# A relational graph layer on one core: a relu moved to VectorE, one-hots moved into the table stage, 15 scattered tiles, a new order

## The chip, the core and the metric

The kernel runs on one core of one Trainium2 chip. A core has TensorE (PE, matrix products, which accumulate in PSUM), VectorE (DVE), ScalarE (ACT), GpSimd (POOL, which here mostly issues indirect DMAs), SyncE (SP, which issues the other DMAs) and 16 DMA engines. Each engine works through its own instructions in their written order; semaphores let it wait for others. The metric is the time of the whole program on the device in microseconds, the median of several runs. A profile is one execution; its span reaches from the first to the last instruction.

## What is computed

A graph with 625 nodes and 20625 edges (each drawn edge both ways, and a loop at every node), sorted by target, four kinds of edge, 512 features. In short:

```python
h = relu(layernorm(x))
for r in range(4):
    msg += (h[src] @ W_rel[r] + b_rel[r]) * where(edge_type == r, edge_weight, 0)
agg = segment_sum(msg, dst) / maximum(segment_sum(edge_weight, dst), 1)
x1  = layernorm(h + h @ W_self + b_self + agg) * g1 + b1
ffn = gelu(x1 @ W_ffn1 + b_ffn1) @ W_ffn2 + b_ffn2
out = x + layernorm(x1 + ffn) * g2 + b2
```

## The kernel before, in words

The nodes lie in five blocks of 128 rows (0 and 4 are called outer, 1 to 3 inner). The edges lie in 162 tiles of 128, sorted by target, so each tile reaches one or two blocks.

**Table stage.** Each block is centred and passed through a relu (`pre_norm`, the rest of the norm is a scale that follows later), transposed on TensorE (L406), copied to SBUF by ScalarE (L412), and multiplied with each of the four `W_rel`: 20 steps, `step = r * NB + i`, one table row of 128 x 512 each (`table_rows`, L463, eight passes on TensorE in fp32). In the steps of the first kind the next block's transposes stand in the middle of a row's products. VectorE scales each product, adds the bias (the eviction, L476) and SP stores it to `table` in DRAM. In `pre_norm` blocks 0 and 1 take their relu on VectorE (L427), blocks 2 to 4 on ScalarE (L423, L424). The relu of block `i + 3` is written behind step `i`, block 2's ahead of step 0.

**Outer blocks.** The edges of the outer blocks are not gathered. Their weights are summed into matrices (edges of one kind and source block against target), which multiply the table rows. Most of these tiles are scattered to DRAM cells: VectorE sums equal neighbours (`line_sums`, L732 to L740, eight columns at a time), GpSimd issues one indirect DMA for each tile (`scatter`, L746), and the matrix of each outer block is loaded back later (`load_sums`, L766, into `sums_w`). `LINES = 999, 16` gives the most tiles that are scattered for block 0 (31 here) and block 4 (16). The remaining outer tiles go through one-hots on VectorE (`node_hots`, L641 and L651, named `os` and `od`), scaling on ScalarE (L659, `ohw`) and short products (L673), a few of them already at steps 15 to 17.

**Degrees and first edges.** Weighted degrees come from bf16 one-hots (`degree_hots`, L839) times weights. Those of the 30 inner groups are made at steps 8 and 9; from them come counts (L972) and, on TensorE, the group in which each inner block's first edge stands (`first_edges`, L903 to L907, `x_group`, at step `FIRST_AT = 16`). GpSimd then loads these edges (`load_first_edges`, L911). The one-hots of the 72 outer degree tiles are made in two instructions behind the last table row (`outer_degree_hots`), in the memory of the feed-forward's two `gT` buffers.

**Edge stage.** GpSimd gathers the table row of every inner edge tile (L1313, 99 of them, and three first edges, L1391) into ten `ms` buffers. Three neighbouring tiles form a group: ScalarE weights the first (L1319), VectorE adds the next two (L1349), the sum is split in a high part (ScalarE, L1323) and a low part (VectorE, L1327), and TensorE adds both to the targets by a one-hot (L1374). In between TensorE has the self products (L501), the outer blocks' sums over the table (L1490, 40 of them, most on rows that SP loads back, L1485), the transposes (L406) and the feed-forward (L1055, L1075). The last block's norm and feed-forward end the program.

**What sets the order.** In the table stage the order is that of the written loop with its step constants. In the edge stage each piece of work is an `op` of a planner, and `ORDER`, a table of op numbers, is the order in which they are written out on all engines. GpSimd's stream is: the scatters as their weights come, at `FIRST_AT` the three loads, the last five scatters, an instruction that waits for the stored rows (L761), then the gathers.

Of the kernel before, what the change touches and what calls it, by code (L numbers as in the profile page):

```python
# [9 lines left out]
F32 = mybir.dt.float32  # L10
F32R = mybir.dt.float32r
I32 = mybir.dt.int32
BF16 = mybir.dt.bfloat16
# [3 lines left out]
P = 128  # L17
# [1 line left out]
NEAR = 63  # L19
PAUSE = 200  # L20
PIECE = 8
LINES = 999, 16


class EdgePlan:
# [48 lines left out]


ORDER = [
# [30 lines left out]
]  # L107


# [92 lines left out]
def gnn_layer(ctx, tc, x, edges, edge_line, edge_groups, w_self, w_rel, w_ffn1, w_ffn2, rows_in, bf_in, out, n_edges):  # L202
# [12 lines left out]
    nc = tc.nc  # L215
# [11 lines left out]
    NC = R * NB  # L227
# [191 lines left out]
    rx = const.tile([P, NB, 3], F32, name="rx")  # L419

    def pre_norm(i, mean):
        if i > 1:
            nc.scalar.activation(rx[:, i, 2:3], mean, AF.Copy, scale=-1.0)  # L423
            nc.scalar.activation(z[:, i, :], xs[:, i, :], AF.Relu, bias=rx[:, i, 2:3])  # L424
        else:
            for c in (slice(0, D // 2), slice(D // 2, D)) if i == 0 else (slice(0, D),):
                nc.vector.tensor_scalar(z[:, i, c], xs[:, i, c], mean, 0.0, op0=ALU.subtract, op1=ALU.max)  # L427
        nc.vector.tensor_scalar(rx[:, i, 0:1], var_of[i], EPS, None, op0=ALU.add)
        rsqrt_pow(rx[:, i, :])
# [138 lines left out]
    sums_w = {}  # L568
# [193 lines left out]

    def load_sums(i):
        b = lines[i][0]
        sums_w[b] = const.tile([P, NC, P], F32, name=f"sums_w{b}")
        load = (nc.sync if i else nc.scalar).dma_start(  # L766
            sums_w[b], cells[i][:P * NC * P, :].rearrange("(p c n) o -> p c (n o)", p=P, c=NC))
        if i:
            wait_for(load, made_row[-1:], "rows go first")
        wait_for(load,  # L770
                 scattered[i][:-1], "all cells are there")

    rdeg = const.tile([P, NB], F32, name="rdeg")
    W = ep.width
    starts = early.tile([P, -(-NT // 8), 8], F32, name="starts")
# [83 lines left out]
    dg = early.tile([4, NP], F32, name="dg")  # L859

    box_dg = {}

    def outer_degree_hots(j0, nj, oc):
        oc.append(buffer("gT").rearrange("p f q -> p (f q)").bitcast(BF16)[:, :nj * W].rearrange("p (j w) -> p j w", w=W))
        degree_hots(j0, nj, oc[0])

    def outer_degree_sums(j0, nj, oc):

        upper = ep.first[outer_blocks[2]] - 2 * P
        for j in range(j0, j0 + nj):  # L870
            s = ep.starts[deg_tiles[j]]
            lo, hi = max(s, 0), min(s + W, N)
            low = deg_tiles[j] < GROUP0
# [2 lines left out]
            if j == GROUPS:  # L876
                box_dg["p"] = buffer("ps")
                nc.tensor.matmul(box_dg["p"][:4, :], zeros[:, :4], zeros, start=True, stop=False)
            nc.tensor.matmul(box_dg["p"][:4, at:at + hi - lo], w3[:, j, :], oc[0][:, j - j0, lo - s:hi - s],
                             start=False, stop=j == ND - 1)  # L880

    def outer_degree_copy():
# [269 lines left out]
    FIRST_PIECE = 4  # L1152
    COLUMNS_AT, LINE_AT, DEGREE_HOTS_AT = (0, 2, 4, 7, 10, 12, 14), 9, (8, 9)
    COLUMNS_OF_EDGES_AT, LOAD_AT, LIMITS_AT = 5, 16, (3, 6)
    DEGREES_AT, SPREAD_AT, FIRST_AT = 13, 15, 16
    chunks = [(j0, min(DG, GROUPS - j0)) for j0 in range(0, GROUPS, DG)]
    ODG = -(-(ND - GROUPS) // GT)
    outer_chunks = [(j0, min(ODG, ND - j0)) for j0 in range(GROUPS, ND, ODG)]
    later_groups = [(a, min(2, NE - a)) for a in range(0, NE, 2)]
    pieces = [(0, 0, FIRST_PIECE)]  # L1160
# [20 lines left out]
    with tc.manual_schedule(engines={PE, DVE, ACT, mybir.EngineType.Pool}):  # L1181
# [12 lines left out]
        for r in range(R):  # L1194
            for i in range(NB):
# [26 lines left out]
                if step in DEGREE_HOTS_AT:  # L1222
                    j0, nj = chunks[DEGREE_HOTS_AT.index(step)]
                    hots.append((step, degree_hots(j0, nj, early.tile([P, nj, W], BF16, tag="oc", name=f"oc_{j0}", bufs=2))))
                if step in ADDS_AT:
                    for b in range(*((0, 2), (2, 4), (4, NB))[ADDS_AT.index(step)]):
                        nc.vector.tensor_add(xs[:, b, :], xs[:, b, :], b2_bc)
# [51 lines left out]

    rows_of_first = op("DVE", 2.2, first_rows, rank=(0.3,), level=0.2)  # L1280
    first_ready = op("DVE", 2.7, first_found, after=[rows_of_first], rank=(0.3,), level=0.2)
    degree_op, hots_ops = None, []
    for j0, nj in outer_chunks:
        oc = []
        h = op("DVE", 1.6, lambda j0=j0, nj=nj, oc=oc: outer_degree_hots(j0, nj, oc), take=["gT"], rank=(0.3,), level=0.2)
        first_sum = degree_op is None
        degree_op = op("PE", 0.028 * nj + 0.1, lambda j0=j0, nj=nj, oc=oc: outer_degree_sums(j0, nj, oc),
                       after=[h, degree_op], take=["ps"] if first_sum else [], give=[("gT", h)], lag=0.25, rank=(2, 0.05), level=0.3)
        sum_op = degree_op if first_sum else sum_op
    degree_op = op("ACT", 0.6, outer_degree_copy, after=[degree_op], take=["ow"], give=[("ps", sum_op)],  # L1290
                   rank=(2, 0.05))
    spread_op = op("PE", 0.4, outer_degree_rows, after=[degree_op], take=["ps"], give=[("ow", degree_op)], lag=0.25, rank=(2, 0.05), level=0.3)
    degree_op = op("DVE", 0.55, outer_degrees, after=[spread_op], give=[("ps", spread_op)], rank=(0.3,), level=0.2)
# [196 lines left out]
        nc.tensor.matmul(acc[b,], sums_w[b][:, c, :], kept[(b, c) if (b, c) in kept else c], start=first, stop=last)  # L1490

    landed = op("cells", CELLS, None)
    banked, before_ = [op("SP", 0.3, lambda: load_sums(1), after=[landed], lag=6.5, rank=(0, -1))], None
    for i, (k0, n_) in enumerate(later_groups):
        box = {}
        rank = (0.55, i)
# [273 lines left out]
```

## Time and profile before

| | |
|---|---|
| median of 3 runs | 259.22 us (258.03 to 260.24) |
| profiled execution | 259.05 us, its span 257.3 us |
| busy in the span: PE / DVE / ACT / POOL | 240.7 / 198.6 / 107.1 / 171.3 us |
| PE weight loads busy | 141.7 us |
| table stage on PE | 6.0 to 85.9 us |
| gathers issued on POOL | 92.7 to 225.7 us |
| DMA, mean over the span | 231 GB/s |

Times inside the profile count from the start of the span. In a row of the timeline stand the start, the busy time, the engine, the line, the operation with output and input, their sizes, the number of merged instructions, and in brackets the idle time of the engine ahead of it with what ended it; "issue" there means that nothing in the profile was waited for. A row of stretches gives for each engine the busy time and the number of instructions, then TensorE's granted clock (1.00 is full), the DMA engines' share and GB/s. Groups of the page list the line, the engine, the operation, the count, the busy time with the mean of one in ns, and the idle time ahead of them. PE is TensorE's products, PEld its weight loads, which lie beside them.

### The profile page before, as it was taken

Reading aid. Unit: us, or ns where it says so; the run is one execution under the profiler, and the core shown is the slowest. Engines: PE = TensorE matmul, PEld = TensorE weight load, DVE = VectorE, ACT = ScalarE, POOL = GpSimd, SP = SyncE. Lnnn points to the kernel's source line nnn. Section 1 sums busy time; section 2 is a strip of 40 time slices with the busy share of each in tenths; the row PEclk is TensorE's granted clock in tenths of the full one; section 3 lists DMA queues with packets and bytes.
Section 4 is the critical chain, followed back from the end, with each engine's and each line's share of the span. In section 5 each row is a group of like instructions: output and inputs, shape, how many; then the busy total and the mean of one; then the engine's idle time right before and its main releaser. Section 6 shows DMA issues by size and latency. Waiting matters only on the chain.

```text
span 257.3 us, 3583 instructions
## 1 busy us (share of the span) xinstructions
PE 240.7 (94%) x1049; PEld 141.7 (55%) x1049; DVE 198.6 (77%) x471; ACT 107.1 (42%) x328; POOL 171.3 (67%) x232
## 2 busy tenths in 40 slices
PE   7699999999989997999999998999996999899992
PEld 7245444444444663446454556666766748647871
DVE  2756699999897991699997979998695994977342
ACT  3132900000033001977462447855646672652540
POOL 5385588688888877877777677777777777701000
PEclk9979999999999999999999999999999999999998
DMA  5999899786263259998999977766777667821111
GB/s 179 349 408 406 318 347 326 283 311 248 85 203 127 83 158 338 384 349 302 300 321 357 321 201 207 206 200 197 199 213 206 202 204 206 241 87 41 43 41 43
DMA packets 24030, 59.44 MB, mean 231 GB/s; under 512 B 4452, under 2 KB 8776, under 8 KB 22855
## 3 DMA queue, kind: packets, MB, share of 16 engines
q0 software_dynamic: 9760, 26.79, 33.9%
q1 hardware_dynamic: 13920, 30.91, 33.6%
q10 hardware_dynamic: 326, 1.48, 1.7%
q8 instruction: 9, 0.15, 0.2%
q14 instruction: 15, 0.11, 0.1%
HBM read 49.99 MB, written 9.17 MB: 230 GB/s over the span
## 4 chain that ended last, share of the span: by engine, by line
PE 52%; DVE 17%; DMA 15%; issue 5%; POOL 4%; ACT 4%; SPq 1%; DVEq 0%; POOLq 0%; ACTq 0%
PE ps L463 24%; DMA ms<-table,row_i 12%; PE acc L1490 7%; PE ps L1055 6%; PE acc L1374 5%; PE ps L501 4%; POOL ms L1313 4%; PE ps L1075 3%; DVE add L1349 3%; DMA line<-in_edge_line_dram 2%; DVE z L489 2%; DVE gT L839 1%; DVE oh L1366 1%; DVE el L1327 1%; PE ps L406 1%
## 5 line engine op out<-in xcount | busy, mean ns | idle before, releaser
L1313 POOL DMA_INDIRECT ms<-table,row_i x99 | 98.5, 994 | 31.5 <-issue 14.0
L463 PE MATMUL ps<-wr,T 128*128 128x512 f32 (+2 forms) x168 | 72.8, 587 | 2.5 <-ACT T L412 2.5
L746 POOL DMA_INDIRECT cells<-weight,cell x47 | 49.2, 1046 | 14.8 <-DVE weight L740 7.6
L463 PEld LDWEIGHTS ps<-wr,T 128*128 128x128 f32 x168 | 31.3, 195 | 37.5 <-issue 30.7
L1349 DVE SCALAR_TENSOR_TENSOR add<-ms,wgt_g,add 128x512 f32<-128x512 f32 x55 | 40.4, 751 | 8.4 <-DMA ms<-table,row_i 5.1
L1055 PEld LDWEIGHTS ps<-T,w_sb 128*128 128x128 f32 x320 | 39.0, 191 | 5.8 <-issue 2.4
L1055 PE MATMUL ps<-T,w_sb 128*128 128x128 f32 (+2 forms) x320 | 39.7, 275 | 1.4 <-ACT gT L1061 1.1
L1075 PE MATMUL ps<-w_sb,gT 128*128 128x512 f32 (+2 forms) x96 | 37.0, 523 | 0.1
L1490 PE MATMUL acc<-tr,sums_w 128*128 128x512 f32 x60 | 29.5, 597 | 0.0
L1319 ACT ACTIVATE add<-ms,wgt_g 128x512 f32<-128x512 f32 x30 | 20.6, 689 | 19.0 <-DVE el L1327 13.8
L1075 PEld LDWEIGHTS ps<-w_sb,gT 128*128 128x128 f32 x96 | 16.4, 190 | 12.5 <-issue 9.8
L1374 PE MATMUL acc<-eh,oh 128*128 128x512 f32 x34 | 17.5, 530 | 5.1 <-ACT eh L1323 2.0
L1327 DVE TENSOR_TENSOR el<-add,eh 128x512 fp32r<-128x512 f32 x25 | 17.0, 684 | 4.9 <-ACT eh L1323 2.9
L1323 ACT CAST eh<-add 128x512 fp32r<-128x512 f32 x25 | 14.6, 584 | 12.3 <-DVE add L1349 12.2
L501 PE MATMUL ps<-ws_sb,T 128*128 128x512 f32 x40 | 18.8, 597 | 0.0
L659 ACT ACTIVATE ohw<-os,w 128x128 fp32r<-128x128 f32 x32 | 10.2, 389 | 19.4 <-DVE os L641 19.4
L1061 ACT ACTIVATE gT<-ps,bf 128x128 f32<-128x128 f32 (+1 forms) x40 | 13.9, 360 | 10.1 <-PE ps L1055 9.8
L476 DVE SCALAR_TENSOR_TENSOR tr<-ps,rx,brel_bc 128x512 f32<-128x512 f32 x15 | 11.1, 745 | 8.0 <-PE ps L463 5.9
L1374 PE MATMUL acc<-el,oh 128*128 128x512 f32 x34 | 17.1, 512 | 0.0
L1490 PEld LDWEIGHTS acc<-tr,sums_w 128*128 128x128 f32 x60 | 10.8, 189 | 8.3 <-issue 7.4
L1337 ACT ACTIVATE eh<-ms,ed 128x512 fp32r<-128x512 f32 x9 | 6.3, 712 | 21.0 <-issue 16.7
L1374 PEld LDWEIGHTS acc<-eh,oh 128*128 128x128 f32 x34 | 6.4, 189 | 12.6 <-ACT eh L1337 4.2
(250 smaller groups left out, 310.2 us busy)
## 6 DMA issues: line engine op xcount, KB each, us to landing
tr<-table SPq DMA_DIRECT2D x11, 512.0 KB, 6.2
w_sb<-in_L_gnn_W_ffn_dram SPq DMA_DIRECT2D x2, 2048.0 KB, 8.0
table<-tr SPq DMA_DIRECT2D x15, 256.0 KB, 2.8
wr<-in_L_gnn_W_rel_dram SPq DMA_DIRECT2D x3, 1024.0 KB, 7.4
cells<-zeros SPq DMA_DIRECT2D x2, 1280.0 KB, 8.2
ms<-table,row_i POOLq DMA_INDIRECT x99, 3.9
rows<-in_rows_dram SPq DMA_DIRECT2D x1, 1280.0 KB
sums_w<-cells ACTq DMA_DIRECT2D x1, 1280.0 KB
```

The source lines that it names most:

```text
L463: nc.tensor.matmul(p_[:, :h.stop - h.start], hT[i][:, k, :], wr_sb[r][:, k, h], start=(k == 0), stop=(k == KD - 1))
L501: nc.tensor.matmul(p[0], hT[i][:, k, :], ws_sb[:, k, :], start=(k == 0), stop=(k == KD - 1))
L746: s = nc.gpsimd.indirect_dma_start(out=cells[i][:, :], out_offset=bass.IndirectOffsetOnAxis(ap=cell[i][:, k:k + 1], axis=0), in_=weight[i] ...
L1055: nc.tensor.matmul(pu[:, low:nn + first], w1_sb[:, k, f * P:(f + 1) * P], x1T_b()[:, k, low:nn + first], start=(k == 0), stop=(k == KD - 1))
L1075: nc.tensor.matmul(po[h][:n, :w], box["gT"][:, f, at], w2_sb[:, f, c], start=(f == 0), stop=(f == KF - 1))
L1313: nc.gpsimd.indirect_dma_start(out=ms[j], out_offset=None, in_=table[:, :], in_offset=bass.IndirectOffsetOnAxis(ap=row_i[:, j:j + 1], axis=0))
L1319: nc.scalar.activation(box["sum"], ms[j], AF.Copy, scale=wgt_g[:, (j - GROUP0) // EG, 0:1])
L1323: nc.scalar.copy(box["high"], box["sum"])
L1327: nc.vector.tensor_sub(box["low"], box["sum"], box["high"].bitcast(F32))
L1349: nc.vector.scalar_tensor_tensor(to, ms[j], wgt_g[:, k, q:q + 1], box["sum"], op0=ALU.mult, op1=ALU.add)
L1374: nc.tensor.matmul(acc[bs], w.bitcast(F32) if of.dtype == F32 else w, of, start=first, stop=last)
L1490: nc.tensor.matmul(acc[b,], sums_w[b][:, c, :], kept[(b, c) if (b, c) in kept else c], start=first, stop=last)
```

## The change

Four things change. Block 2's relu is taken on VectorE like those of blocks 0 and 1. At most 15 tiles of block 4 are scattered instead of 16, so one tile more goes through one-hots. The outer degrees' one-hots are made at steps 17 and 18 of the table stage, in the memory of the second outer block's matrix (`sums_w`, which is now allocated for both blocks ahead of the stages), the 72 degree products become one op, and the second matrix's load comes behind that op. `FIRST_AT` goes from 16 to 17. `ORDER` is another table of the same 699 numbers (three ops go with the outer one-hots, three come with the 17th one-hot tile).

```diff
-LINES = 999, 16
+LINES = 999, 15
...
 ORDER = [
-    401, 403, 406, 411, 25, 2, 440, 27, 4, 441, 404, 405, 407, 32, 442, 420, 443, 408, 414, 3, 26, 28, 444, 5, 445, 6,
+    398, 400, 403, 408, 440, 441, 401, 7, 22, 0, 402, 404, 24, 2, 407, 23, 25, 29, 8, 3, 409, 1, 442, 34, 39, 443,
...
     def pre_norm(i, mean):
-        if i > 1:
+        if i > 2:
             nc.scalar.activation(rx[:, i, 2:3], mean, AF.Copy, scale=-1.0)
...
+    for b, _, _ in lines:
+        sums_w[b] = const.tile([P, NC, P], F32, name=f"sums_w{b}")
...
-    def outer_degree_hots(j0, nj, oc):
-        oc.append(buffer("gT").rearrange("p f q -> p (f q)").bitcast(BF16)[:, :nj * W].rearrange("p (j w) -> p j w", w=W))
-        degree_hots(j0, nj, oc[0])
-
-    def outer_degree_sums(j0, nj, oc):
+    outer_hots = sums_w[lines[1][0]].rearrange("p c n -> p (c n)").bitcast(BF16)[:, :(ND - GROUPS) * W].rearrange(
+        "p (j w) -> p j w", w=W)
+
+    def outer_degree_sums():
...
-    DEGREES_AT, SPREAD_AT, FIRST_AT = 13, 15, 16
+    DEGREES_AT, SPREAD_AT, FIRST_AT, OUTER_HOTS_AT = 13, 15, 17, (17, 18)
...
+                if step in OUTER_HOTS_AT:
+                    j0, nj = outer_chunks[OUTER_HOTS_AT.index(step)]
+                    degree_hots(j0, nj, outer_hots[:, j0 - GROUPS:j0 - GROUPS + nj, :])
...
-    banked, before_ = [op("SP", 0.3, lambda: load_sums(1), after=[landed], lag=6.5, rank=(0, -1))], None
+    banked, before_ = [op("SP", 0.3, lambda: load_sums(1), after=[landed, sum_op], lag=6.5, rank=(0, -1))], None
```

How the instructions stand on their engines before and after is read from the programs; numbers behind names are buffer numbers.

ScalarE, at the start of the table stage: `T_152` to `T_154` are the transposed blocks 0 to 2, `z` a block's relu. Rows with a minus are of before, rows with a plus of after.

```order
 L412 COPY T_152<-ps_80 128x2x128
-L423 ACTIVATE rx<-mv_x_284 128x1
-L424 ACTIVATE z<-xs,rx 128x512
 L412 COPY T_153<-ps_78 128x4x128
-L423 ACTIVATE rx<-mv_x_304 128x1
+L423 ACTIVATE rx<-mv_x_305 128x1
 L424 ACTIVATE z<-xs,rx 128x512
 L412 COPY T_154<-ps_80 128x4x128
```

The copy of block 1 (`T_153`) no longer stands behind block 2's relu; the copy of block 2 still stands behind block 3's.

VectorE, at steps 16 and 17 of the table stage, before: `m` is an evicted row, `xs` the input with a bias added.

```order
L476 SCALAR_TENSOR_TENSOR m_798<-ps_78,rx,brel_bc 128x512
L1227 TENSOR_TENSOR xs<-xs,rows 128x512 x2
L641 TENSOR_TENSOR os_199<-key,node_row 128x256
L651 TENSOR_SCALAR od_201<-node_row,key 128x280
L651 TENSOR_SCALAR od_202<-node_row,key 128x260
L907 TENSOR_SCALAR x_group<-ps_79 128x3
L476 SCALAR_TENSOR_TENSOR m_835<-ps_80,rx,brel_bc 128x512
```

The same place after, from step 16's eviction to step 18's:

```order
L476 SCALAR_TENSOR_TENSOR m_797<-ps_78,rx,brel_bc 128x512
L1229 TENSOR_TENSOR xs<-xs,rows 128x512 x2
L641 TENSOR_TENSOR os_201<-key,node_row 128x256
L651 TENSOR_SCALAR od_203<-node_row,key 128x280
L651 TENSOR_SCALAR od_1_198<-node_row,key 128x500
L476 SCALAR_TENSOR_TENSOR m_814<-ps_79,rx,brel_bc 128x512
L840 TENSOR_TENSOR sums_w_186<-rel,row_w 128x1368
L1229 TENSOR_TENSOR xs<-xs,rows 128x512 x2
L641 TENSOR_TENSOR os_200<-key,node_row 128x256
L651 TENSOR_SCALAR od_204<-node_row,key 128x260
L651 TENSOR_SCALAR od_205<-node_row,key 128x260
L906 TENSOR_SCALAR x_group<-ps_80 128x3
```

`x_group` has moved behind the next eviction (`m_814`), half of the outer one-hots (`sums_w_186`) and that step's adds and one-hots. On GpSimd only the count of the scatters ahead of the three loads changes, from 11 of block 4's to 10; five follow the loads as before.

TensorE, around the first product with a gathered edge (`acc_2 <- eh, oh`), before:

```order
L1490 MATMUL acc_910<-m_760,sums_w_801 128x512
L1490 MATMUL acc_910<-m_798,sums_w_801 128x512
L1490 MATMUL acc_910<-m_835,sums_w_801 128x512
L1374 MATMUL acc_2_1062<-eh_889,oh_902 128x512
L1490 MATMUL acc_910<-m_869,sums_w_801 128x512
L889 MATMUL ps_79<-ident,ow_896 128x4 x4
L501 MATMUL ps_81<-ws_sb,T_152 128x512 x2
```

After:

```order
L501 MATMUL ps_81<-ws_sb,T_152 128x512 x2
L673 MATMUL ps_79<-od_204,ohw_208 128x260 x2
L1485 MATMUL acc_908<-tr_609,sums_w_185 128x512
L1485 MATMUL acc_908<-tr_662,sums_w_185 128x512 x2
L1369 MATMUL acc_2_1040<-eh_889,oh_902 128x512
L673 MATMUL ps_79<-od_205,ohw_208 128x260 x2
L1485 MATMUL acc_908<-tr_731,sums_w_185 128x512
```

Block 0's four self products (L501, here the second pair) have moved ahead of the first edge product, and five of the ten products of block 0's sum (L1490, now L1485) that stood ahead of it have moved behind.

More of the change, by code (lines that the diff above doesn't have):

```diff
@@ L764, in load_sums @@
         b = lines[i][0]
-        sums_w[b] = const.tile([P, NC, P], F32, name=f"sums_w{b}")
         load = (nc.sync if i else nc.scalar).dma_start(
@@ L861, in gnn_layer @@
     box_dg = {}
-    def outer_degree_hots(j0, nj, oc):
-        oc.append(buffer("gT").rearrange("p f q -> p (f q)").bitcast(BF16)[:, :nj * W].rearrange("p (j w) -> p j w", w=W))
-        degree_hots(j0, nj, oc[0])
-    def outer_degree_sums(j0, nj, oc):
+    outer_hots = sums_w[lines[1][0]].rearrange("p c n -> p (c n)").bitcast(BF16)[:, :(ND - GROUPS) * W].rearrange(
+        "p (j w) -> p j w", w=W)
+    def outer_degree_sums():
         upper = ep.first[outer_blocks[2]] - 2 * P
-        for j in range(j0, j0 + nj):
+        for j in range(GROUPS, ND):
             s = ep.starts[deg_tiles[j]]
@@ L878, in outer_degree_sums @@
                 nc.tensor.matmul(box_dg["p"][:4, :], zeros[:, :4], zeros, start=True, stop=False)
-            nc.tensor.matmul(box_dg["p"][:4, at:at + hi - lo], w3[:, j, :], oc[0][:, j - j0, lo - s:hi - s],
+            nc.tensor.matmul(box_dg["p"][:4, at:at + hi - lo], w3[:, j, :], outer_hots[:, j - GROUPS, lo - s:hi - s],
                              start=False, stop=j == ND - 1)
@@ L1154, in gnn_layer @@
     COLUMNS_OF_EDGES_AT, LOAD_AT, LIMITS_AT = 5, 16, (3, 6)
-    DEGREES_AT, SPREAD_AT, FIRST_AT = 13, 15, 16
+    DEGREES_AT, SPREAD_AT, FIRST_AT, OUTER_HOTS_AT = 13, 15, 17, (17, 18)
     chunks = [(j0, min(DG, GROUPS - j0)) for j0 in range(0, GROUPS, DG)]
-    ODG = -(-(ND - GROUPS) // GT)
+    ODG = -(-(ND - GROUPS) // len(OUTER_HOTS_AT))
     outer_chunks = [(j0, min(ODG, ND - j0)) for j0 in range(GROUPS, ND, ODG)]
@@ L1281, in gnn_layer @@
     first_ready = op("DVE", 2.7, first_found, after=[rows_of_first], rank=(0.3,), level=0.2)
[L1282 to L1290, printed above, removed]
+    sum_op = op("PE", 0.028 * (ND - GROUPS) + 0.2, outer_degree_sums, take=["ps"], lag=0.25, rank=(2, 0.05), level=0.3)
+    degree_op = op("ACT", 0.6, outer_degree_copy, after=[sum_op], take=["ow"], give=[("ps", sum_op)],
                    rank=(2, 0.05))
```

58 rows, old and new, of the table ORDER are left out of this document.

## The prediction

> **What bounds the kernel now.** I read the clock and span first, then GpSimd's timeline, then the waits of TensorE, VectorE and ScalarE where GpSimd or TensorE stands still. The profiled execution took 259.05 us, its span 257.3, so 1.75 us lie outside it; the median of the three runs, 259.22, is 0.17 above it.
>
> ```profile
> core 0: 257.3 us, clock 0.990
> 92.73 0.98 POOL L1313 DMA_INDIRECT ms<-table,row_i  x1 [0.76 <-DVE x_step L919]
> 127.15 0.94 POOL L1313 DMA_INDIRECT ms<-table,row_i  x1 [0.49 <-ACT add L1319]
> 132.33 0.94 POOL L1313 DMA_INDIRECT ms<-table,row_i  x1 [0.42 <-DVE add L1349]
> 147.38 0.94 POOL L1313 DMA_INDIRECT ms<-table,row_i  x1 [0.87 <-DVE add L1349]
> 224.71 0.94 POOL L1313 DMA_INDIRECT ms<-table,row_i  x1 [0.30 <-issue]
> 234.31 0.61 PE L406 MATMUL ps<-ident,z 128*128 128x128 f32 x4
> 101.00:235.00 134.00, 128.70 (x567) 80.31 (x566) 111.04 (x208) 78.60 (x201) 95.86 (x97) 1.00 0.76 241
> ```
>
> From the first gather at 92.73 to the last of 102 (99 edge tiles, 3 first edges) at 224.71, GpSimd issues one every 131.98/101 = 1.31 us; an undisturbed one is 0.94 busy behind 0.30 of issue, about 1.25. Only three waited for anything, 0.49, 0.42 and 0.87 instead of 0.30: 0.9 us in all. So the edge stage runs at GpSimd's pace, and the end is that stream's start, plus 132.9, plus a tail of 31.7 us that the last edges' sum, norm and feed-forward fill (the last block's transposes stand 9.6 us behind the last gather's issue). TensorE is nearly full beside it: busy for 128.70 of 134 us (the columns are PE, its weight loads, VectorE, ScalarE, GpSimd), 5.3 us free. So the question is when the stream starts, and whether TensorE keeps up.
>
> The start hangs on GpSimd's scatters, and these on VectorE:
>
> ```profile
> 50.59 0.96 POOL L746 DMA_INDIRECT cells<-weight,cell  x1 [1.94 <-DVE weight L740]
> 80.06 1.36 POOL L911 DMA_INDIRECT x_edges<-in_edge_groups_dram,x_group  x1 [0.17 <-DVE m L476]
> 86.84 2.07 POOL L746 DMA_INDIRECT cells<-weight,cell  x1 [0.17 <-issue]
> 89.22 1.19 POOL L746 DMA_INDIRECT cells<-weight,cell  x1 [0.17 <-issue]
> 90.71 0.97 POOL L746 DMA_INDIRECT cells<-weight,cell  x1
> ```
>
> Behind the wait at 50.59 GpSimd never stops: 22 scatters up to 80.06 (29.47 us, 1.34 each), three loads of the first edges, five scatters, the first gather.
>
> **Block 2's relu.**
>
> ```profile
> 7.79 0.49 DVE L427 TENSOR_SCALAR z<-xs,mv_x 128x512 f32<-128x512 f32 x1
> 8.33 0.66 PE L406 MATMUL ps<-ident,z 128*128 128x128 f32 x4 [0.21 <-DVE rx L428]
> 8.83 2.09 PE L463 MATMUL ps<-wr,T 128*128 128x512 f32 x4
> 11.75 0.18 DVE L439 BATCH_NORM_AGGREGATE mv_x<-st_x 128x2 f32<-128x6 f32 x1
> 12.20 0.72 ACT L424 ACTIVATE z<-xs,rx 128x512 f32<-128x512 f32 x1
> 12.83 0.57 ACT L412 COPY T<-ps 128x512 f32<-128x512 f32 x1
> 13.45 3.54 PE L463 MATMUL ps<-wr,T 128*128 128x512 f32 x4 [2.52 <-ACT T L412]
> 14.00:15.00 1.00, 1.00 (x2) 0.50 1.08 389
> 13.93 0.72 ACT L424 ACTIVATE z<-xs,rx 128x512 f32<-128x512 f32 x1
> 16.06 0.42 DVE L740 TENSOR_REDUCE weight<-same 128x4 f32<-128x256 f32 x1
> 19.26 0.75 DVE L476 SCALAR_TENSOR_TENSOR tr<-ps,rx,brel_bc 128x512 f32<-128x512 f32 x1 [2.78 <-PE ps L463]
> 21.10 0.72 ACT L424 ACTIVATE z<-xs,rx 128x512 f32<-128x512 f32 x1
> 24.57 0.60 PE L406 MATMUL ps<-ident,z 128*128 128x128 f32 x4
> ```
>
> Block 1's transposes end at 8.99, but their copy stands on ScalarE behind block 2's relu until 12.83. TensorE waits 2.52 us and then runs at a granted clock of 0.50 (the column behind the busy time of that stretch): four passes, half a table row, take 3.54 us. At full clock they would take half, 1.77, so the half clock costs as much again.
>
> [...]
>
> After the change the copy needs only the transposes, so block 1's row starts behind block 0's, at 10.92. VectorE's relu takes 0.49 behind the aggregate that ends at 11.93: 12.42, in time for the transposes at 10.92 + 1.77 = 12.69. But ScalarE still has block 3's relu ahead of block 2's copy, and VectorE reaches it 0.49 later: 13.93 + 0.72 + 0.49 = 15.1, with the copy 15.7, a wait of about 0.9 for TensorE. Block 4's relu is ahead of block 3's copy: the scatter's first weights end at 16.48 + 0.49 = 16.97; from the next eviction to that relu's end is 21.82 - 19.26 = 2.56, and the copy 0.57: 20.1, a wait of about 0.5. Neither is near 2.52. Block 4's transposes come at 20.1 + 1.77 = 21.9 instead of 24.57: TensorE gains 2.7 us. VectorE's work up to 66 us follows the rows, so the scatter weights move with it, and GpSimd's 50.59 becomes 47.9. VectorE's extra 0.49 lies before its wait for rows at 19.26 and costs nothing behind it.
>
> **One scattered tile less.** One of the 22 scatters goes: GpSimd comes to the first edges' loads at 80.06 - 2.7 - 1.3 = 76.1. The tile becomes a 17th one-hot tile: one more `od` on VectorE, two scalings on ScalarE, two short products. By the stretch from 101 to 235 there are 23 us free on VectorE, 55 on ScalarE and 5.3 on TensorE for under 1 us each: nothing.
>
> **First edges a step later, one-hots in the last rows.**
>
> ```profile
> 66.23 0.75 DVE L476 SCALAR_TENSOR_TENSOR tr<-ps,rx,brel_bc 128x512 f32<-128x512 f32 x1 [1.00 <-PE ps L463]
> 74.35 0.39 PE L903 MATMUL ps<-counts,before 128*128 128x3 f32 x2 [0.69 <-DVE counts L972]
> 74.98 0.75 DVE L476 SCALAR_TENSOR_TENSOR m<-ps,rx,brel_bc 128x512 f32<-128x512 f32 x1
> 77.77 0.14 DVE L907 TENSOR_SCALAR x_group<-ps 128x3 int32<-128x3 f32 x1
> 79.87 1.28 DVE L1227 TENSOR_TENSOR xs<-xs,rows 128x512 f32<-128x512 f32 x2
> 82.05 0.32 DVE L535 TENSOR_TENSOR lim<-fl,lim 128x162 f32<-128x162 f32 x1
> 86.49 3.08 DVE L839 TENSOR_TENSOR gT<-rel,row_w 128x1368 bf16<-128x1368 bf16 x2
> ```
>
> The loads of the first edges need `x_group`. VectorE writes it now behind one more eviction, the first half of the outer one-hots and that step's adds. From the eviction that waits for TensorE: 66.23 - 2.7 = 63.5; to the eviction of two steps on 8.75, less 0.4 for seven columns instead of eight: 71.9; on to where `x_group` stood 2.8, with 0.2 for longer `od`: 74.9; the eviction 0.7, half of the one-hots 1.54, the adds and `od` from 79.87 to 82.05 2.2: 79.3, and 0.14. So GpSimd, there at 76.1, waits 3.4 us and goes on at 79.6, only 0.5 before 80.06. Behind it stand the five scatters and the whole gather stream. What the scatters at 86.84 and 89.22 took over 0.97, 1.3 us, came while the one-hots ran; one half of these now falls into the wait, which saves between 0 and 1.3; I take half, 0.6. The first gather: 92.73 - 0.5 - 0.6 = 91.6.
>
> [...]
>
> VectorE's last eviction was ahead of 86.49; with 3.08 more before it and 2.7 gained it comes by 86.9 at the latest, well ahead of 91.6, so the last row's store is hidden. Behind it VectorE is rid of the 3.08 where it soon waited for gathers: nothing. TensorE no longer waits 0.69 for the counts, but will wait for gathers instead: nothing. Its degree products lie ahead of the first gathers before and after: nothing. The second matrix's load waits for them now, but stands on SP behind two table loads that need buffers TensorE holds until later: nothing.
>
> **The refitted order** has no row before. Its bounds are, below, the 0.9 us of gather waits and part of the 131.98 - 101 x 1.25 = 5.7 us by which gathers ran long, and above, TensorE's 5.3 free, if they are lost. I take 0, the stream as it was.
>
> Sum: 257.3 - 1.1 = 256.2 of span, 257.95 with 1.75; on the median's scale 258.1.
>
> **Rivals.**
>
> ```profile
> 85.91 1.02 PE L1490 MATMUL acc<-m,sums_w 128*128 128x512 f32 x2
> 100.25 0.50 PE L1374 MATMUL acc<-eh,oh 128*128 128x512 f32 x1 [1.32 <-ACT eh L1337]
> 159.28 0.47 PE L1374 MATMUL acc<-eh,oh 128*128 128x512 f32 x1 [1.12 <-DVE z L489]
> 198.97 0.50 PE L1374 MATMUL acc<-eh,oh 128*128 128x512 f32 x1 [2.05 <-ACT eh L1323]
> 199.00:200.00 1.00, 1.00 (x8) 1.00 0.78 254
> 219.42 2.94 PE L1055 MATMUL ps<-T,w_sb 128*128 128x128 f32 x24 [1.06 <-ACT gT L1061]
> ms<-table,row_i POOLq DMA_INDIRECT x99, 3.9
> ```
>
> *The order gives more.* The gather waits go (0.9), and a sixth of the other 4.8 us of long gathers: 258.1 - 1.7 = 256.4. Were `x_group` also ready when GpSimd gets there, up to 3.4 more. For it: one-hots and norms now stand ahead of the gathers. Against it: the stream hardly waited.
>
> *TensorE becomes the bound.* Its table rows end at 85.91 - 2.7 - 0.69 = 82.5. Ahead of the first edge product it had 13.0 us of work, to 98.93, and now one large product (0.9) less: it is through at 94.6. The first gather's product comes 4.6 us (3.9 of landing, 0.7 on ScalarE) to 7.5 us (as before) behind its issue, at 96.2 to 99.1. If the wait reaches 2.52 us, the point that decides, the half clock costs 1.8. Then 128.7 + 1.3 (the product and the tile) + 1.8 from 99.1, with the waits of 1.12, 2.05 and 1.06 for gathers and activations, end at 235.1, not at 234.31 - 1.1: 260.0. Against it: few transfers meet the first gather, so it may land in time.
>
> *The first stop stays.* If block 3's relu holds ScalarE so that TensorE stops for as long as before, nothing moves early, `x_group` comes at 79.44 + 2.7 = 82.1, and the first gather 2.2 - 0.6 = 1.6 us later than before: 260.8. It decides from an early gain under 1.6 us. Against it: the two new waits come out at 0.9 and 0.5.
>
> **How the numbers follow.** Forecast 0.53 (257 to 259.4), more from the order 0.26, TensorE 0.13, no early gain 0.08. Eight in ten: 1 us below the first rival's time, for part of its 3.4, gives 255.4; the last rival gives 260.8. The three runs lie 2.2 us apart, so 1% (2.6 us) is about what can be told from no change. Under 256.6 lie most of the first rival and the forecast's edge, 0.26; over 261.8 only the tails of the last two, 0.06; between them 0.68.
>
> **What would show it.** Right: no half clock and no wait over 1 us on TensorE from 9 to 24 us; GpSimd waiting some 3 us for `x_group` near 79.6; the first gather at 91 to 92, the last 132 later. Wrong: a first gather before 90 or after 93, gathers that wait over 2 us in all, a granted clock of 0.50 near 97, or a tail outside 31 to 32.5.

## The result, and the profile after

| | before | after |
|---|---|---|
| median of 15 runs each, side by side | 258.44 us (256.57 to 260.24) | 261.17 us (259.69 to 262.93) |
| after / before | | 1.011, 95% interval 1.008 to 1.014 |
| profiled execution, span | 259.05, 257.3 us | 259.69, 257.8 us |
| busy PE / DVE / ACT / POOL | 240.7 / 198.6 / 107.1 / 171.3 us | 241.5 / 198.6 / 106.4 / 169.3 us |

The change makes the kernel about 1.1% slower, 2.7 us. The forecast was 258.1, between 255.4 and 260.8. The profile of after is the fastest of its 15 runs, that of before lies above its median. Seven of the runs further on fell on two slower chips, where every kernel, before included, took 308 to 327 us; their times are not set beside the others.

Clock and span of after, then rows of its timeline, by engine:

```profile
core 0: 257.8 us, clock 0.980
8.64 0.66 PE L406 MATMUL ps<-ident,z 128*128 128x128 f32 x4 [0.94 <-DVE rx L428]
15.54 1.98 PE L463 MATMUL ps<-wr,T 128*128 128x512 f32 x4 [0.63 <-ACT T L412]
21.66 0.60 PE L406 MATMUL ps<-ident,z 128*128 128x128 f32 x4
...
47.66 0.96 POOL L746 DMA_INDIRECT cells<-weight,cell  x1 [1.94 <-DVE weight L740]
79.28 1.21 POOL L910 DMA_INDIRECT x_edges<-in_edge_groups_dram,x_group  x1 [3.37 <-DVE x_group L906]
82.05 1.68 POOL L910 DMA_INDIRECT x_edges<-in_edge_groups_dram,x_group  x1 [0.30 <-issue]
91.78 1.07 POOL L1308 DMA_INDIRECT ms<-table,row_i  x1 [1.34 <-issue]
221.59 0.95 POOL L1308 DMA_INDIRECT ms<-table,row_i  x1 [0.30 <-DVE add L1344]
...
96.27 0.50 PE L1369 MATMUL acc<-eh,oh 128*128 128x512 f32 x1 [2.58 <-ACT eh L1332]
231.85 0.61 PE L406 MATMUL ps<-ident,z 128*128 128x128 f32 x4
...
99.00:100.00 1.00, 0.80 (x2) 0.70 (x3) 0.00 (x0) 0.15 (x1) 0.69 (x2) 0.50 0.98 389
```

Up to the last block's transposes, after is ahead. Block 4's transposes come at 21.66 instead of 24.57, the scatter that waits for the weights at 47.66 instead of 50.59, the first gather at 91.78 instead of 92.73, and the last block's transposes at 231.85 instead of 234.31. The 2.46 us won there are lost behind them: from the transposes to the end after takes 257.8 - 231.85 = 25.95 us, before 257.3 - 234.31 = 22.99. This stretch is called the end stretch below.

What VectorE waits for in that stretch, first before, then after (what waits and for what, the sum in us, how often, the longest):

```profile
DVE ow L1100 <- ACT rs_y L995: 5.0, 1, 5.0
DVE ow L1085 <- DMA out_dram<-ow: 2.2, 1, 2.2
DVE ow L1095 <- DMA out_dram<-ow: 0.7, 1, 0.7
```

```profile
DVE ow L1099 <- ACT rs_y L994: 5.5, 2, 4.8
DVE ow L1094 <- DMA out_dram<-ow: 3.8, 1, 3.8
DVE ow L1084 <- DMA out_dram<-ow: 2.2, 1, 2.2
```

A wait for an output store ends when the buffer that is being stored may be written again: in after the store from 235.37 takes 3.73 us, to 239.10, and VectorE writes the buffer from 239.19 on. Before has two as well, but they cost next to nothing. The timeline of before, on VectorE and TensorE:

```profile
248.47 0.56 DVE L1085 TENSOR_TENSOR ow<-ps,z 128x384 f32<-128x384 f32 x1 [2.17 <-DMA out_dram<-ow]
249.60 0.29 DVE L1085 TENSOR_TENSOR ow<-ps,z 128x128 f32<-128x128 f32 x1
249.40 3.00 PE L1401 MATMUL spin<-zeros 128*128 128x256 bf16 x20
```

Spins are products on zeros whose result nobody reads, written behind TensorE's last product; so that product ends where they begin, at 249.40. The second piece of the last block's sum needs it and starts at 249.60, so the store held up only the first piece. In after the two waits stand in one chain. Its pieces in order of time (start, duration, what):

```profile
234.59 0.76 DVE ow L1099
235.37 3.73 DMA out_dram<-ow
...
239.19 0.75 DVE ow L1094
...
241.43 0.17 DVE rs_y L986
241.62 0.21 ACT rs_y L992
...
243.37 0.73 ACT gT L1060 x3
244.12 1.28 ACT L1602
...
246.40 1.43 DVE ow L1099 x2
247.84 2.05 DMA out_dram<-ow
...
250.02 0.57 DVE ow L1084
```

VectorE normalises block 1 (234.59), and SP stores it. The next step, block 4's centring (L1094), writes into the buffer that is being stored, so VectorE stands until 239.19. Behind it stand block 3's variance and the first guess of its root (L986, 241.43). ScalarE has that root's refinement ahead of the last three gelus (243.37) and of the table load for the last square root (1.28 us from 244.12). So block 3's last step is late (246.40), and so are block 4's right behind it (the row holds both) and block 4's store. The last block's first sum (250.02) writes into the buffer of that store. TensorE's spins begin at 247.49 in after, 10.3 us ahead of the end; in before it was 7.9.

The order of after's program shows why. VectorE, behind the last edge product, from block 1's last step on; `ow_896` to `ow_899` are the four buffers:

```order
L1099 SCALAR_TENSOR_TENSOR ow_899<-ow_897,rs_y_0_1898,xs 128x512
L1094 SCALAR_TENSOR_TENSOR ow_899<-ow_898,mv_y_0_1835,rows 128x512
L386 BN_AGGR mv_y_0_2024<-st_y_0_1991 128x2
L391 TENSOR_SCALAR rs_y_0_2026<-mv_y_0_2024 128x1
L1094 SCALAR_TENSOR_TENSOR ow_897<-ow_896,mv_y_0_2024,rows 128x512
L1600 TENSOR_SCALAR rows<-rows 128x512
L985 TENSOR_SCALAR rs_y_0_2026<-rs_y_0_2026 128x1
```

The second row overwrites what the first has just given to a store. In the planner the store is an op of 0.0 us, whose buffers come back at once; in the profile it takes 2.05 and 3.73 us.

### The profile page after: what moved, and what is told of

It is laid out like the page before. It is cut to its first block, busy times and chain, and to the rows that moved or that the text cites. A ratio compares the mean times of both kernels' runs of the same rounds, so it can differ in the third digit from the quotient of the medians.

```text
span 257.8 us, 3594 instructions
## 1 busy us (share of the span) xinstructions
PE 241.5 (94%) x1051; PEld 141.5 (55%) x1051; DVE 198.6 (77%) x474; ACT 106.4 (41%) x328; POOL 169.3 (66%) x230
## 4 chain that ended last, share of the span: by engine, by line
PE 64%; DVE 13%; DMA 10%; ACT 4%; POOL 4%; issue 3%; SPq 1%; POOLq 0%; DVEq 0%
PE ps L463 16%; PE ps L1054 11%; PE ps L1074 11%; PE acc L1485 10%; PE acc L1369 8%; PE ps L501 4%; DMA tr<-table 3%; DMA line<-in_edge_line_dram 2%; DMA out_dram<-ow 2%; DMA ms<-table,row_i 2%; POOL cells L746 2%; POOL x_edges L910 1%; DVE ow L1099 1%; PE ps L673 1%; PE ps L406 1%
## 5 line engine op out<-in xcount | busy, mean ns | idle before, releaser
L1308 POOL DMA_INDIRECT ms<-table,row_i x99 | 97.1, 981 | 31.2 <-issue 16.0
L463 PE MATMUL ps<-wr,T 128*128 128x512 f32 (+2 forms) x168 | 71.3, 577 | 0.8 <-ACT T L412 0.8
L746 POOL DMA_INDIRECT cells<-weight,cell x46 | 47.7, 1036 | 10.7 <-issue 6.4
L463 PEld LDWEIGHTS ps<-wr,T 128*128 128x128 f32 x168 | 30.4, 190 | 35.7 <-issue 29.2
L1485 PE MATMUL acc<-tr,sums_w 128*128 128x512 f32 x60 | 31.2, 623 | 0.5 <-DMA tr<-table 0.5
L1369 PE MATMUL acc<-eh,oh 128*128 128x512 f32 x34 | 16.3, 511 | 3.3 <-ACT eh L1332 3.3
L501 PE MATMUL ps<-ws_sb,T 128*128 128x512 f32 x40 | 18.6, 592 | 0.0
L1485 PEld LDWEIGHTS acc<-tr,sums_w 128*128 128x128 f32 x60 | 10.8, 194 | 8.1 <-issue 5.5
L1336 DVE SCALAR_TENSOR_TENSOR el<-ms,ed,eh 128x512 fp32r<-128x512 f32 x9 | 6.6, 747 | 9.1 <-ACT eh L1332 9.1
```

The costliest lines, as they stand in the source:

```text
L463: nc.tensor.matmul(p_[:, :h.stop - h.start], hT[i][:, k, :], wr_sb[r][:, k, h], start=(k == 0), stop=(k == KD - 1))
L501: nc.tensor.matmul(p[0], hT[i][:, k, :], ws_sb[:, k, :], start=(k == 0), stop=(k == KD - 1))
L746: s = nc.gpsimd.indirect_dma_start(out=cells[i][:, :], out_offset=bass.IndirectOffsetOnAxis(ap=cell[i][:, k:k + 1], axis=0), in_=weight[i] ...
L1308: nc.gpsimd.indirect_dma_start(out=ms[j], out_offset=None, in_=table[:, :], in_offset=bass.IndirectOffsetOnAxis(ap=row_i[:, j:j + 1], axis=0))
L1369: nc.tensor.matmul(acc[bs], w.bitcast(F32) if of.dtype == F32 else w, of, start=first, stop=last)
```

## The experiments

Each kernel was timed in rounds beside the kernel before; ratios are to those runs, with their 95% intervals. Off the slower chips the kernel before had medians of 258.06 to 258.74 us, so medians of different rounds compare to about 0.3%.

**The old order behind the last edge product.** Only the last numbers of `ORDER` differ from after.

```diff
-... 358, 392, 393, 397, 518, 519, 520, 378, 521, 631, 522, ... 636, 675, 677, 604, 659, 674, 664, 683, 679, 676, 660, ...
+... 358, 392, 393, 604, 631, 632, 397, 655, 518, 519, 603, ... 659, 606, 669, 671, 660, 670, 673, 675, 672, 677, 664, ...
```

> The changed kernel, but behind the last edge product the steps stand in the order of the kernel before (the last ten microseconds of work before the end and what leads to them; the work and the buffers' number are the same). Theory 'the refitted tail loses it': in the profile after, VectorE waits 3.84 us for an output store whose buffer it takes again, ScalarE's three last gelus stand behind that wait, and a second store wait of 2.20 us ends the path; the last turned block to the end takes 25.8 us against 23.0 before. Then this run is some 2 to 3 us under the changed kernel, near 258.5, and that stretch takes 23.0 us again. Rival 'TensorE at half clock loses it' (seven microseconds at half clock from 97 to 104): no change here, 261. Second rival, the edge stage's order: no change here.

Measured: 257.98 us, ratio 0.9986 (0.9956 to 1.0015), 3.2 us under after. The end stretch is 22.98 us in its profile. The first theory holds.

**The same order, other buffers.** The centred rows of blocks 4 and 3 go to gather buffers that are free by then; the ops take and give back buffers accordingly.

```diff
-                got["a"] = buffer("ow")
+                got["a"] = buffer("spare" if name in (together[1][0], together[-2][0]) else "ow")
...
+    own_buffers["spare"] = own_buffers["ms"][MS - 2:]
```

> The changed kernel with the same instructions in the same order on every engine; only the buffers differ: the centred rows of two blocks behind the last edge product go to two gather buffers that nobody uses any more, instead of to ow buffers from which a store is still under way. Theory 'the loss is the two store waits that the refitted order brings': both waits of VectorE (2.4 to 3.8 us and 2.2 us) go, the last turned block to the end takes about 23.0 us, and the time falls by about 3 us, to 258. Rival 'it is the order itself' (three gelus behind the norm's root steps on ScalarE, whatever VectorE waits for): that stretch stays above 24 us and the time above 260.

> The run spare once more, since its chip took 314 us for the changed kernel too. Where the kernel before takes 258 us, the theory 'the loss is the two store waits' gives 258 and 23 us from the last turned block to the end; the rival 'it is the order itself' gives 260 or more.

The first run fell on a slower chip. There its profile has no store wait and an end stretch of 22.74 us. The second took 257.56 us, ratio 0.9978 (0.9949 to 1.0008), 3.6 us under after. VectorE's waits behind the transposes in that run, and rows of its timeline:

```profile
DVE ow L1099 <- ACT rs_y L994: 6.0, 2, 5.4
DVE ow L1084 <- PE ps L1074: 1.5, 2, 0.9
```

```profile
91.72 1.06 POOL L1308 DMA_INDIRECT ms<-table,row_i  x1 [1.34 <-issue]
222.93 0.94 POOL L1308 DMA_INDIRECT ms<-table,row_i  x1 [0.31 <-issue]
232.41 0.61 PE L406 MATMUL ps<-ident,z 128*128 128x128 f32 x4
240.54 7.12 PE L1074 MATMUL ps<-w_sb,gT 128*128 128x384 f32 x32
245.92 0.56 DVE L1084 TENSOR_TENSOR ow<-ps,z 128x384 f32<-128x384 f32 x1 [0.86 <-PE ps L1074]
```

No store is waited for, the 32 products run through, and VectorE waits for TensorE instead. The end stretch takes 255.5 - 232.41 = 23.09 us. The instructions stand exactly as in after, so it is the waits, not the order of ScalarE's steps. (Since the two centred rows take no `ow` buffers, the last block's sum goes to block 1's buffer, stored long before, and no longer to block 4's.)

**After once more, unaltered.**

> The changed kernel itself once more, unaltered, beside the others of this call. Median near 261. What it tells is its second profile: if the loss sits in the store waits at the end, the stretch from the last turned block to the end is again 24.5 us or more against 22.8 to 23.1 in every run with the old order there, with a wait of VectorE for an output store of 2 us or more at the same two places. If that stretch is 23 us here, the tail isn't the cause.

> The changed kernel unaltered once more, since its first repeat ran on a chip on which every kernel took 310 to 319 us. Median near 261; from the last turned block to the end 24.5 us or more, with VectorE's waits for output stores in it. If that stretch is 23 us, the tail isn't the cause.

Both fell on the slower chips (313.27 us, ratio 1.002, and 314.53, ratio 0.990), so their times say nothing about the median. Their profiles show the two waits again, 4.5 and 2.2 us, and 4.2 and 2.2 us; the end stretch takes 26.9 and 26.4 us, where spare took 22.74 on the chip of the second. Over all runs of this document the four profiles with the refitted end and its buffers have 24.6 to 26.9 us there, the sixteen others 22.7 to 23.3.

**Products on zeros ahead of the first edge product.** After, with 16 bf16 products in the place of the 2.58 us wait.

```diff
         if first:
             acc[bs] = ps_acc.tile([P, D], F32, tag="acc", name=f"acc{bs[0]}_{len(bs)}")
+            [nc.tensor.matmul(acc[bs][:, :D // 2], zeros[:, D // 2:D // 2 + P], zeros[:, D // 2:], start=True, stop=True) for _ in range(16 * (bs == order_of[0]))]
```

> The changed kernel with 16 extra products on zeros ahead of the first edge product on TensorE, where the profile after has a wait of 2.58 us and behind it the half clock to 104 us; nothing else moves. Theory 'half clock': seven microseconds at 0.5 are 3.5 us of TensorE's work, and TensorE is busy almost without a stop from 104 to 248, so the time falls by 2 to 3.5 us, to about 258 to 259. Rival 'the refitted tail loses it', with GpSimd's gathers setting the edge stage as in the kernel before: the gathers never waited for TensorE, so the time stays within 0.5 us of 261.2.

> The two edits of the runs tail and warm together on the changed kernel: the old order behind the last edge product, and 16 products on zeros ahead of the first one. If the lost store waits at the end and the half clock at 97 us are two separate losses, their gains add: 261.2 less 3.2 less 2.2 is 255.8. If they are two views of one loss (the time that one gives back the other can't), the time stays at 257.5 to 258.5.

Alone they gave 259.00 us, ratio 1.0046 (1.0014 to 1.0077): 2.2 us under after by the medians, 0.6% by the ratios, whose intervals just touch. With the old order at the end it is 257.81, ratio 0.9987 (0.9958 to 1.0016), against 257.98 and 0.9986 without them. The clock is 1.00 from 92 to 232 us in warm, and in tail_warm from 94 to 112 and in the mean of the whole span. So the half clock is worth nothing measurable once the store waits are gone, and the gains don't add. What the products give back alone seems to belong to the same loss: in that profile the first store wait is 2.4 us instead of 3.8, and the end stretch 24.55. Why the store landed sooner there, and whether it does so always, stays open.

**The relu alone.** The kernel before with `if i > 2`.

> The kernel before with one edit, block 2's relu on VectorE; scatters, one-hots and order stay. Theory of the prediction: the 2.52 us wait of TensorE for ScalarE's copy goes, and the half clock behind it, the table is stored 2.7 us earlier and the gathers start as much earlier: 255.7. Rival: the start of the gathers is set by GpSimd's scatters and not by the stores once those are earlier, or what is gained is lost again behind (a cold TensorE before the first edge product): 257.5 to 258.5.

Measured: 255.41 us (255.07 to 255.90), ratio 0.990 (0.987 to 0.994). Its timeline:

```profile
90.23 0.98 POOL L1313 DMA_INDIRECT ms<-table,row_i  x1 [0.76 <-DVE x_step L919]
221.34 0.95 POOL L1313 DMA_INDIRECT ms<-table,row_i  x1 [0.30 <-issue]
231.28 0.61 PE L406 MATMUL ps<-ident,z 128*128 128x128 f32 x4
```

The gathers start 2.50 us earlier than before, take 131.11, and the end comes 3.2 us earlier (span 254.1). This one edit beats both kernels, before by 1.0% and after by 2.0% by the ratios.

**All parts in the old order.** After, with before's `ORDER`, the steps of the 17th one-hot tile put in beside their neighbours (that placement is mine).

> All parts of the change but the refitted order: the 699 steps stand in the order of the kernel before, the steps of the 17th one-hot tile put in beside their neighbours and the last rows' one-hot sums taken from the second matrix's memory. Theory 'the refitted order loses what the parts gain': 255.5 to 256.5, the sum of the prediction. Theory 'half clock before the first edge product, whatever the order': 258 to 260. Theory 'the parts themselves cost': 261.

> The run oldorder (259.5) with one constant back: the first edges' group numbers are worked out at step 16 as in the kernel before, not 17. GpSimd's wait of 3.37 us for x_group goes. Theory 'the later step costs': the last scatters and the first gather come some 3 us earlier (first gather at 89 instead of 92.0), TensorE no longer stops for 2.5 us ahead of the first edge product, and the time falls by 2.5 to 3.5 us, to 256 to 257. Rival 'the table's last store holds the first gather': it starts at 91 or later as before and the time falls by under 1 us.

> The run oldorder (259.5) with the 16 products on zeros ahead of the first edge product; the first gather stays at 92.0. Theory 'half clock': the run oldorder shows clock tenths of 5 behind a wait of 2.47 us, and without them the time falls by about 2 us, to 257.5. Rival 'gathers' pace': with the old order TensorE has slack behind 104 us that takes the half clock in, and the time stays within 0.5 us of 259.5.

> Both edits on the run oldorder: x_group at step 16 and 16 products on zeros. If the later step and the cold TensorE that follows it are the whole of what the other parts of the change lost against the relu alone (255.4), this run is at 255.4 or, with one scatter less (1.27 us of GpSimd), at 254 to 255. If it stays at 257 or above, the 17th one-hot tile or the one-hots' move costs something by itself.

The edit of old_first is one constant:

```diff
-    DEGREES_AT, SPREAD_AT, FIRST_AT, OUTER_HOTS_AT = 13, 15, 17, (17, 18)
+    DEGREES_AT, SPREAD_AT, FIRST_AT, OUTER_HOTS_AT = 13, 15, 16, (17, 18)
```

| | median | ratio to before |
|---|---|---|
| oldorder | 259.46 us | 1.0060 (1.0023 to 1.0097) |
| with `x_group` at step 16 (old_first) | 257.82 us | 0.9979 (0.9935 to 1.0023) |
| with the products on zeros (old_warm) | 260.46 us | 1.0103 (1.0042 to 1.0165) |
| with both (old_first_warm) | 256.97 us | 0.9959 (0.9925 to 0.9993) |

The old order did not bring 255.5 to 256.5. It is 4 us over the relu alone, with an end stretch of 22.96 us, so the other parts cost something of their own in this order. The refitted order up to the last edge product is better for them than the old one with my placement: tail, which has it, took 257.98. The products on zeros don't help here either. The earlier `x_group` does, by 1.6 us (0.8% by the ratios, whose intervals touch), but most of its gain is lost on the way. GpSimd and VectorE in old_first:

```profile
89.77 0.98 POOL L1308 DMA_INDIRECT ms<-table,row_i  x1 [1.34 <-issue]
106.49 1.21 POOL L1308 DMA_INDIRECT ms<-table,row_i  x1 [1.68 <-DVE el L1336]
131.62 0.94 POOL L1308 DMA_INDIRECT ms<-table,row_i  x1 [1.15 <-DVE add L1344]
222.91 0.95 POOL L1308 DMA_INDIRECT ms<-table,row_i  x1 [0.30 <-DVE add L1344]
...
DVE od L651 <- PE ps L673: 7.9, 3, 5.0
```

The first gather comes 2.3 us earlier than in oldorder (92.03), the last only 0.7 (223.58): the stream takes 133.14 us, with gathers that wait for VectorE. VectorE stands for 7.9 us in all (5.0 the longest) ahead of one-hots (`od`) whose buffers TensorE's short products still read; those are among the steps that I placed, and relu_hots_c below, with 16 tiles scattered, has no such wait.

**`x_group` at step 16 in the refitted order, and the one-hots' move alone.** The first is the run tail with the constant above. The second is relu_only with the one-hots' move (`LINES` 16, old order).

> The run tail (258.0) with x_group at step 16 again. Theory 'the later step and the tail order are two separate losses': 1.6 us less as from oldorder to old_first, so 256.4. Rival 'TensorE and the landing of the first gathers set the edge stage in the refitted order': within 0.5 us of 258.0.

> The run relu_only (255.4) with one part more: the last rows' one-hots made at steps 17 and 18 into the second matrix's memory and summed in one go; 16 tiles are scattered as before, the order is that of the kernel before, x_group at step 16. The run old_first is this kernel with 15 tiles scattered (257.8). Theory 'the one-hots' move costs' (3.1 us of VectorE ahead of the last table tiles, fewer products for TensorE while it waits for the first gather): 257 to 258. Theory 'the 17th one-hot tile costs': 255.4, and the 2.4 us come with the 15 tiles.

> The run tail (258.0) with x_group at step 16, repeated for the same reason. Two separate losses: 256.4. Rival 'TensorE and the landing of the first gathers set the edge stage': within 0.5 us of 258.0.

> The run relu_only (255.4) with the one-hots' move alone (16 tiles scattered, old order, x_group at step 16), repeated for the same reason. If the move costs: 257 to 258. If the 17th one-hot tile costs: 255.4, since the run old_first, which has 15 tiles scattered besides, took 257.8.

> The run tail with x_group at step 16, on a chip where the kernel before takes 258 us. Two separate losses: 256.4. Rival 'TensorE and the landing of the first gathers set the edge stage': within 0.5 us of 258.0.

> The run relu_only (255.4) with the one-hots' move alone, on a chip where the kernel before takes 258 us. If the move costs: 257 to 258. If the 17th one-hot tile costs: 255.4, since old_first, which has 15 tiles scattered besides, took 257.8.

The first two runs of each fell on the slower chips (312.0 to 316.4 us), with intervals of about 1% and more; they decide nothing. The third ones, tail_first_c and relu_hots_c: 257.21 us, ratio 0.9954 (0.9912 to 0.9996), and 256.27, ratio 0.9924 (0.9893 to 0.9955). The first is under tail by 0.3% with overlapping intervals, less than the 1.6 us I had added up: its gathers start at 89.59 and end at 222.77, where spare, with the same order up to the last edge product, starts at 91.72 and ends at 222.93. Tail's own profile, from its slowest run (260.15 us), has 92.51 and 225.93; beside that one both ends would have moved by about 3 us, which the medians don't show. The second isn't told apart from the relu alone (0.9903): 0.2% with overlapping intervals, so the one-hots' move costs nothing that can be told here. Between it and old_first lies only block 4's 16th tile, scattered in the one and a one-hot tile in the other: 0.6% with intervals that overlap. Whether one scatter less costs anything stays open, but it brought nothing.

## Why the prediction was wrong

**The step that failed** is "The refitted order ... I take 0, the stream as it was", and with it the tail of 31.7 us that the sum carried over. I bounded the order by the gather waits and by TensorE's free time in the edge stage, and looked at the new order in the places of the other parts alone. It also reorders the norms behind the last gather. From the end of the last gather's issue to the end of the span, after takes 257.8 - 222.54 = 35.3 us. Of the 3.6 more, 2.96 lie behind the transposes, and they are the two store waits: spare takes these away with the instructions in the same order, and comes to 257.56 with a tail of 31.6 us. The other 0.65 lie between the last gather and the transposes (9.31 us in after, 8.66 in before, 8.54 in spare); why is open. The prediction named a tail outside 31 to 32.5 as what would prove it wrong, but no rival carried it, and the range's upper end had none of it. No row of before showed the new wait; the order of the new program did, in two neighbouring rows, and the 2.17 us wait for a store, which the prediction did not look at, gave a first price (3.84 and 2.20 in after).

**The rest of the sum came out, the rule behind it only in part.** Without the store waits the kernel takes 257.56 (spare) or 257.98 (tail), where the forecast was 258.1. Term by term:

- *The relu*: 2.7 us for TensorE at block 4's transposes, measured 2.91. The two waits for ScalarE's copies were named as 0.9 and 0.5 and are 0.63 (15.54) and 0.16 us. The 0.94 at 8.64 is another one, block 1's transposes waiting for VectorE, 0.21 in before. The clock is 1.00 in the mean from 9 to 24 us, where before has 0.89. Alone the relu brings 2.8 us of the median (255.41 beside 258.23).
- *`x_group` and the scatters*: a wait of 3.4 us and a start at 79.6, measured 3.37 and 79.28. Of the 1.3 us that slow issues took beside the one-hots, the prediction kept half; in after one load of the first edges took 1.68 us (82.05) beside the second half of the one-hots (81.34 to 82.91), 0.73 over the 0.95 of the one ahead of it, and the scatters behind them 0.96 to 1.00. What makes an issue slow there no run shows. The first gather: 91.6, measured 91.78. The hit is partly luck: the loads start 0.3 us early, and the idle time ahead of the first gather is 1.34 us where before had 0.76, a term that the sum did not have.
- *The stream*: 132 us. In after's profile, its fastest run, 129.81, in the same order with other buffers (spare) 131.21.
- *That the end follows the stream's start* holds for the relu (the first gather 2.5 us earlier, the last 3.4, the end 3.2) but not for `x_group`: from oldorder to old_first the start moved by 2.3 us and the last gather by 0.7, from spare to tail_first_c by 2.1 and 0.2; both streams took longer (133.14 and 133.18 us). So a total that fits is no proof of this rule.
- *One scatter less*: GpSimd came to the loads at 75.91 where the sum had 76.1, so the scatter's gain was won there. But no run shows it at the end: old_first, with 15 tiles scattered, isn't below relu_hots_c, with 16.

**The rivals.** "TensorE becomes the bound" said 260.0, near the measured time, and its event came: a wait of 2.58 us ahead of the first edge product, and the half clock from 97 to 104 (0.58, then 0.50 or 0.51), which the prediction had also named as a sign of being wrong. But it isn't the cause. Its price was 1.8 us and more; with the store waits out of the way, keeping the clock at 1.00 changes the ratio from 0.9986 to 0.9987 (tail, tail_warm), nothing that can be told. Hitting the time would have been for the wrong reason. "The order gives more" has something to it in the middle of the program (tail against oldorder, 0.7%, intervals just apart, though part of that may be my placement in oldorder); at the end about twice as much was lost. "The first stop stays" did not happen.

## What to carry to other kernels

When a schedule is refitted, read the last stretch first: nothing behind it can take in what it loses. Look there for an instruction that writes a buffer which the instruction ahead of it has handed to a store, and see whether the planner gives that buffer back before the store has landed. And let a change of four parts be timed part by part: here one line of it, alone, beats the whole by 2.0%.

## What the runs showed of the hardware that was not expected

**The clock fell after shorter waits than thought, but not after each.** The prediction took 2.52 us as the point that decides: my estimate, from the wait of before at 13.45; no run shows such a point. On the faster chips the half clock followed waits of TensorE of 1.84 (old_first), 1.85 (oldorder, whose mean clock from 180 to 225 is 0.96), 2.34 (old_first), 2.47 (oldorder), 2.58 (after), 3.04 (tail), 3.27 (spare_c) and 5.08 us (tail_first_c). Waits of 1.88 (warm) and, before, 2.05 us had the clock at 1.00 behind them, and so had one of 1.7 us in relu_only. In old_first, and in tail:

```profile
197.70 0.50 PE L1369 MATMUL acc<-eh,oh 128*128 128x512 f32 x1 [1.84 <-ACT eh L1318]
199.00:200.00 1.00, 1.00 (x5) 0.84 (x4) 1.00 (x2) 0.94 (x5) 0.77 (x1) 0.50 0.77 201
...
97.12 0.50 PE L1369 MATMUL acc<-eh,oh 128*128 128x512 f32 x1 [3.04 <-ACT eh L1332]
97.70 1.70 PE L1485 MATMUL acc<-tr,sums_w 128*128 128x512 f32 x2
102.16 0.79 PE L1369 MATMUL acc<-eh,oh 128*128 128x512 f32 x1 [2.76 <-ACT eh L1332]
```

In tail the second wait came at half clock, 0.50 from 98 to 108, ten microseconds in all. Between 1.84 and 2.05 us the runs went either way, so the length of one wait does not settle it there.

**A store's landing time is not one number.** The same store of block 1 (224 KB from SP, 30 KB from ScalarE; SP's part landed in 3.7 us in after, in 2.3 in warm) held VectorE for 3.8 us in after, 2.4 in warm, and 4.5 and 4.2 in the repeats of after on the slower chips.
